# Row sums of the last two pairs of heads: exponentials of two steps added in place by VectorE

## The chip, the core and the metric

The kernel runs on one core of a Trainium2 chip. The metric is device microseconds (us) of one execution; less is better. The engines are named as the profile names them: PE (TensorE, matmuls), PEld (its weight loads), DVE (VectorE), ACT (ScalarE), POOL (GpSimd) and SP (SyncE, which here only issues DMAs). Each engine works through its own instructions in program order and waits on semaphores for the others. Matmul results stand in PSUM, everything else on the chip in SBUF.

## What is computed

A transformer block on x (2048 tokens of 512): layer norm, causal attention with 16 heads of 32, and a gated feed-forward layer; both results are added to x.

```python
q, k, v = (qkv[0], qkv[1], qkv[2])
scores = jnp.einsum('bhqd,bhkd->bhqk', q, k) * scale
scores = jnp.where(causal, scores, jnp.finfo(scores.dtype).min)
probs = jax.nn.softmax(scores, axis=-1)
attn = jnp.einsum('bhqk,bhkd->bhqd', probs, v)
...
x = x + _L0_attn_ref(xn, ...) + _L0_ffn_ref(xn, ...)
```

The change lies in the softmax's denominator: for each query the exponentials of all its scores have to be summed over the keys.

## The kernel before

**Tiling.** Queries come in 4 blocks of 512 (`qb`), keys in 16 tiles of 128 (`kt`). A *step* is one pair (`qb`, `kt`) of one head pair `p` (two heads; 8 pairs): scores with the 128 keys on partitions and the 512 queries on columns, their exponentials in a tile `prob` of 128 x 2 x 512 (two heads), and two products with them: with the values (`av`) and with a matrix of ones (`rows`), which gives the sums over the keys. Block `qb` has 4 `qb` steps *off the diagonal* (all keys lie before all queries) and 4 *diagonal* ones, d = 0 to 3, in which only 512 - 128 d columns are computed and a 128 x 128 triangle has to be cut out. There are 40 steps (`STEPS`).

**Stages.** After the projections a long loop (from line 820) takes six head pairs through 40 steps each. The stage that the change touches is the next one (lines 857 to 976): the last two pairs, 6 and 7, go through the 40 steps *together*, four heads at a time. Behind it comes the output projection (line 1147), then the feed-forward layer.

**One step of the together stage**, in the order in which it is written out by hand (lines 944 to 968), which is the order of each engine's queue:

- PE: `score_cols` (line 242) and `add_scores` (line 257) put the scores of four heads into four PSUM tiles. Each of the two pairs has three such tiles in rotation (`ps_t`, `ps_s`), two of them in one step, so a step's second tile needs the first exponential of the step before to be done with its own.
- PE: `run_due(s)` issues what earlier steps put off with `later_on(wait, ...)` to this step: `values_together` (line 895, four matmuls on four groups of 32 columns) and `rows_together` (line 909, likewise) of the step before.
- DVE, diagonal steps only: the scores of the triangle are cut at zero (line 880, four instructions).
- ACT: four exponentials (line 881), ordered head 0 of both pairs, then head 1. They write the step's two `prob` tiles, each with two heads.
- POOL, diagonal steps only: the triangle is cut out of each `prob` tile (line 286, two instructions).
- `keep_together`: at a block's end the value sums are copied by ACT (line 924) and the row sums by DVE (line 927); `normalize_attention` (lines 407 and 409: reciprocal on DVE, product on POOL) is done in eighths, one per step.

The order of the steps (`together`, line 861) is, for each block in the order 1, 0, 2, 3: diagonal d, then `qb` steps off the diagonal, for d = 0 to 3. The pool `probs` (line 796) has five buffers; the long loop uses it too, there with one tile per step, and the last matmuls that read such a tile are issued at most four steps after it.

In the long loop POOL already adds the exponentials of two steps (`add_up`, line 352), so that there one row-sum product serves two steps. In the together stage each step has its own.

Of the kernel before, what the change touches and what calls it, by code (L numbers as in the profile page):

```python
# [42 lines left out]
ALU = mybir.AluOpType  # L43
# [3 lines left out]
P = 128  # L47
# [33 lines left out]
def block_kernel(  # L81
# [10 lines left out]
    nc = tc.nc  # L92
# [8 lines left out]
    with (  # L101
# [39 lines left out]
        units, steps, first = [], [], {}  # L141
# [86 lines left out]
        def rows_when_due(beside_values=True):  # L228
            if due and tick[0] >= due[0][0]:
                rows_from_parts(beside_values)  # L230
            tick[0] += 1

        def score_cols(p, n, pool):

            qb, kt = steps[n]
            c0 = max(0, kt - 4 * qb) * P
            tiles = []
            for h in range(2):
                first = rows_of(p, h).start
                rows = slice(first, first + 3)  # L240
                ps = tile_of(pool, f"ps_t{p}_{n}_{h}")
                nc.tensor.matmul(  # L242
                    ps[:, c0:],
                    lhsT=ones_h[rows, :],
                    rhs=negs[p // 2, qb][rows, c0:],
                    start=True,
                    stop=False,
                )
                tiles.append(ps)
            return tiles  # L250

        def add_scores(p, n, tiles):
            qb, kt = steps[n]
            c0 = max(0, kt - 4 * qb) * P
            for h, ps in enumerate(tiles):
                rows = rows_of(p, h)
                nc.tensor.matmul(  # L257
                    ps[:, c0:],
                    lhsT=keys[kt // 4][rows, p // 2, (kt % 4) * P : (kt % 4 + 1) * P],
                    rhs=queries[qb][rows, p // 2, c0:],  # L260
                    start=False,
                    stop=True,
                )
# [21 lines left out]
        def omit_later_keys(diag):  # L285
            nc.gpsimd.affine_select(
                out=diag,
                in_=diag,
                compare_op=ALU.is_ge,
                fill=0.0,  # L290
                base=0,
                pattern=[[0, 2], [1, P]],
                channel_multiplier=-1,
            )
# [80 lines left out]
        def keep_attention():  # L375

            p, qb = full.pop(0)
            av, row = avs[p, qb], rows[p, qb]
            og, half = p // 2, slice(64 * (p % 2), 64 * (p % 2 + 1))
            if p % 2 == 0:  # L380
                sums[og, qb] = sump.tile([P, TB], F32, tag="sums", name=f"sums{og}_{qb}")
            if p >= NP - 2:
                copy = nc.vector.tensor_copy if p % 2 else nc.scalar.copy
                copy(aT[og][qb][half], av[:64])
                copy(sums[og, qb][half], row[64:])
            else:
                if qb == 0:
                    nc.scalar.copy(aT[og][qb][half], av[:64])
                else:
                    both = turn_tile(8 + p % 2, f"both{p}_{qb}")  # L390
                    nc.scalar.copy(both, av)  # L391
                nc.vector.tensor_copy(sums[og, qb][half], row[64:])
                if qb > 0:
                    other = slice(64 * (1 - p % 2), 64 * (2 - p % 2))
                    nc.scalar.copy(aT[og][qb][half], both[other])
                    nc.gpsimd.tensor_tensor(
                        aT[og][qb][half], aT[og][qb][half], both[half], ALU.add
                    )
            if p % 2 == 1:
                invert.extend((og, qb, i) for i in range(8))  # L400

        def normalize_attention():

            og, qb, i = invert.pop(0)
            cols = slice(i * (P // 2), (i + 1) * (P // 2))
            part = sums[og, qb][:, cols]
            nc.vector.reciprocal(part, part)
            dst = aT[og][qb][:, cols]
            nc.gpsimd.tensor_tensor(dst, dst, part, ALU.mult)
# [383 lines left out]
            tc.tile_pool(name="late", bufs=1, side="right", reuse_waits="tile")  # L793
        )
        attention = ExitStack()
        probs = attention.enter_context(tc.tile_pool(name="probs", bufs=5, reuse_waits="tile"))
        sump = attention.enter_context(tc.tile_pool(name="sums", bufs=5, reuse_waits="tile"))

        def turn_tile(i, name, dtype=F32, shape=(P, TB)):
# [13 lines left out]
        def later_on(wait, f, *args):  # L813
            todo.setdefault(at[0] + wait, []).append((f, args))

        def run_due(m):
            for f, args in todo.pop(m, []):
                f(*args)

        for m in range((NP - 2) * STEPS):  # L820
            p, n = divmod(m, STEPS)
# [12 lines left out]
            qb, kt = steps[n]  # L834
# [22 lines left out]
        together = []  # L857
        for qb in TOGETHER:
            mine = [n for n in range(STEPS) if steps[n][0] == qb]
            for d in range(4):  # L860
                together += [mine[4 * qb + d], *mine[d * qb : (d + 1) * qb]]

        def diagonal(n):
            return steps[n][1] >= 4 * steps[n][0]

        def exponentials_together(n, two):

            qb, kt = steps[n]
            c0 = max(0, kt - 4 * qb) * P
            both = [  # L870
                probs.tile([P, 2, TB], F32, tag="prob", name=f"prob{NP - 2 + i}_{n}")
                for i in range(2)
            ]
            for h in range(2):
                for i in range(2):
                    ps = two[i][h]
                    if diagonal(n):

                        diag = ps[:, c0 : c0 + P]
                        nc.vector.tensor_scalar(diag, diag, 0.0, None, ALU.min)  # L880
                    nc.scalar.activation(both[i][:, h, c0:], ps[:, c0:], AF.Exp)
            if diagonal(n):
                for i in range(2):
                    omit_later_keys(both[i][:, :, c0 : c0 + P])
            return both
# [19 lines left out]
        def rows_together(qb, exps, c0, first, last):  # L905
# [10 lines left out]
            if last:  # L916
                kept.append(("rows", qb))

        kept = []

        def keep_together():
            what, qb = kept.pop(0)
            if what == "values":
                nc.scalar.copy(aT[NOG - 1][qb], avs[NP, qb])
            else:
                sums[NOG - 1, qb] = sump.tile([P, TB], F32, tag="sums", name=f"sums_last{qb}")
                nc.vector.tensor_copy(sums[NOG - 1, qb], rows[NP, qb])
                invert.extend((NOG - 1, qb, i) for i in range(8))
# [5 lines left out]
        def load_rest(b, n):  # L934

            lm[b, n] = []
            for part in range(2):
                t = turn_tile(8 * ORDER.index(b) + 2 * n + part, f"lm{b}_{n}_{part}", F32R)
                nc.sync.dma_start(out=t.bitcast(F32), in_=kept_x[b][1 + part][:, n])
                lm[b, n].append(t)  # L940

        early_loads = [(ORDER[i], n) for i in range(2) for n in range(NK)]
        last_n = {steps[n][0]: n for n in together}
        for s, n in enumerate(together):
            at[0] = s
            rows_when_due()
            two = [score_cols(NP - 2, n, ps_t), score_cols(NP - 1, n, ps_s)]
            for i in range(2):
                add_scores(NP - 2 + i, n, two[i])
            if s == 0:  # L950
                for m in sorted(todo):
                    run_due(m)
            run_due(s)
            qb, kt = steps[n]
            both = exponentials_together(n, two)
            while full:
                keep_attention()
            while kept:
                keep_together()
            first = s == 0 or steps[together[s - 1]][0] != qb  # L960
            last = n == last_n[qb]
            later_on(1, values_together, n, both, first, last)
            exps = [both[j // 2][:, j % 2] for j in range(4)]
            later_on(1, rows_together, qb, exps, max(0, kt - 4 * qb) * P, first, last)
            if invert:
                normalize_attention()
            if early_loads and s > 4:
                load_rest(*early_loads.pop(0))
        assert not early_loads
        for m in sorted(todo):  # L970
            run_due(m)
        while kept:
# [117 lines left out]
    for n in range(NG * NC):  # L1090
        g, j = divmod(n + 1, NC)
        pieces += [(g, 0, j), (g, 1, j)] if g < NG else [None, None]
        g, j = divmod(2 * (n // 2 + 1) + n % 2, NC)
# [237 lines left out]
```

## Time and profile before

| what | us |
|---|---|
| three runs | 1923.87, 1920.15, 1920.36 (median 1920.36) |
| the profiled execution, its own time | 1925.87 |
| its span, first to last instruction | 1924.1 |
| the together stage, from its first scores to the first matmul of the output projection | 675.0 to 789.1 |
| mean granted TensorE clock | 0.995 |

How to read it. A line of a timeline gives start, length, engine, source line, operation, output <- inputs, the pattern and the number of merged instructions; in square brackets stands idle time of that engine and what ended it. A 32-bit matmul shows as two records, so the four matmuls of `rows_together` are x8. In a table by windows each engine has its busy time in that stretch. PE matmuls are pipelined: one starts before the record of the last has ended, so the time of a group of matmuls is taken from its start to the start of the next group.

### The profile page before, as it was taken

To read this page: it belongs to the slowest core of one execution; us is meant where nothing else is said; L and a number is where in the kernel's file an instruction comes from. 1 tells how busy PE (TensorE), PEld (TensorE's weight loads), DVE (VectorE), ACT (ScalarE), POOL (GpSimd) and SP (SyncE) were. 2 spreads that over 40 slices of the span, in tenths; PEclk is the share of its full clock that TensorE was granted. 3 is DMA by queue.
4 is the path that set the end of the run, shared out by engine and by line. 5 is a ranking of instruction groups with operands and counts; after the bars stand their busy time and mean duration, and the time that the engine had idled before them with its cause. 6 is when DMAs were issued, how large, how long until landed. Compare 5 with 4: busy or idle time off the path is not lost.

```text
span 1924.1 us, 32421 instructions
## 1 busy us (share of the span) xinstructions
PE 1902.7 (99%) x11981; PEld 1223.0 (64%) x11981; DVE 1325.8 (69%) x2772; ACT 1136.6 (59%) x2364; POOL 945.3 (49%) x1127
## 2 busy tenths in 40 slices
PE   9999999999999999999999999999999999999998
PEld 5666433333333332368888888888888888888886
DVE  7775667776776842348777777677777767777774
ACT  3643466666666666336666666666666666666554
POOL 3310265665665631236555645555555545555551
PEclk9999899999999999999999999999999999999999
DMA  5212000000000110630000000000000000000002
GB/s 197 107 48 88 1 2 2 1 2 2 2 2 2 51 40 2 198 105 24 20 20 21 21 19 21 20 20 20 21 21 19 24 19 19 20 23 19 19 5 88
DMA packets 52991, 65.01 MB, mean 34 GB/s; under 512 B 4960, under 2 KB 37728, under 8 KB 51296
## 3 DMA queue, kind: packets, MB, share of 16 engines
q1 hardware_dynamic: 52832, 62.93, 9.7%
q8 instruction: 94, 1.54, 0.3%
q14 instruction: 65, 0.53, 0.1%
HBM read 46.14 MB, written 16.78 MB: 33 GB/s over the span
## 4 chain that ended last, share of the span: by engine, by line
PE 92%; ACT 3%; POOL 2%; DVE 2%; issue 1%; DMA 0%; SPq 0%; DVEq 0%; ACTq 0%; POOLq 0%
PE gu L1183 25%; PE gu L1196 12%; PE pd L1246 12%; PE ps_s L165 8%; PE av L305 7%; PE pd L1258 6%; PE ps_t L242 4%; PE ps_t L257 3%; PE po L1150 3%; ACT prob L271 2%; PE av_last L895 2%; PE rows_last L909 1%; PE ps_k L592 1%; PE ps_v L592 1%; POOL added L357 1%; PE ps_q L592 1%
## 5 line engine op out<-in xcount | busy, mean ns | idle before, releaser
L1183 PE MATMUL gu<-xh,gu 128*128 128x512 f32 x1024 | 403.9, 394 | 0.0
L1183 PE MATMUL gu<-lm,gu 128*128 128x512 f32 x1024 | 403.6, 394 | 0.0
L189 DVE TENSOR_REDUCE tops<-ps_s 128x1 f32<-128x512 f32 x384 | 245.1, 685 | 112.8 <-PE ps_s L165 74.5
L1267 DVE SCALAR_TENSOR_TENSOR acc<-pd,acc 128x512 f32<-128x512 f32 x512 | 316.9, 680 | 2.4 <-PE pd L1258 2.4
L1228 POOL TENSOR_TENSOR parts<-inter,hi 128x512 fp32r<-128x512 f32 x128 | 171.3, 1338 | 278.8 <-DVE hi L1224 271.1
L165 PE MATMUL ps_s<-k,q 32*128 32x512 f32 (+3 forms) x1280 | 287.3, 583 | 0.0
L1220 DVE SCALAR_TENSOR_TENSOR inter<-gu,gate 128x512 f32<-128x512 f32 x128 | 88.5, 692 | 278.4 <-PE gu L1196 274.2
L1196 PE MATMUL gu<-lm,gu 128*128 128x512 f32 x1024 | 279.7, 395 | 0.0
L257 PE MATMUL ps_t<-q,k 32*128 32x512 f32 (+3 forms) x1280 | 270.5, 540 | 0.0
L1253 ACT ACTIVATE pd<-pd 128x512 f32<-128x512 f32 x512 | 263.2, 581 | 1.1 <-PE pd L1246 1.1
L1190 ACT ACTIVATE gu<-gu 128x512 f32<-128x512 f32 x256 | 148.6, 581 | 187.9 <-PE gu L1183 187.9
L1246 PE MATMUL pd<-wd,parts 128*128 128x512 f32 x1024 | 259.6, 396 | 0.0
L271 ACT ACTIVATE prob<-ps_t 128x512 f32<-128x512 f32 x288 | 156.3, 594 | 119.1 <-PE ps_t L257 95.9
L1196 PEld LDWEIGHTS gu<-lm,gu 128*128 128x128 f32 x1024 | 192.0, 188 | 47.1 <-issue 0.2
L1183 PEld LDWEIGHTS gu<-lm,gu 128*128 128x128 f32 x1024 | 191.9, 187 | 46.6 <-issue 0.2
L1246 PEld LDWEIGHTS pd<-wd,parts 128*128 128x128 f32 x1024 | 192.3, 188 | 45.8
L1183 PEld LDWEIGHTS gu<-xh,gu 128*128 128x128 f32 x1024 | 192.0, 188 | 45.7 <-issue 0.2
L357 POOL TENSOR_TENSOR added<-prob,prob 128x512 f32<-128x512 f32 x144 | 179.6, 1269 | 68.9 <-ACT prob L271 68.4
L305 PE MATMUL av<-prob,v 128*32 128x128 f32 (+3 forms) x1536 | 192.3, 404 | 4.2 <-ACT both L391 2.1
L1227 ACT CAST parts<-hi 128x512 fp32r<-128x512 f32 x128 | 79.8, 623 | 173.7 <-DVE hi L1224 170.2
L1048 POOL TENSOR_TENSOR w<-mag,sc 128x256 f32<-128x256 f16 x128 | 91.9, 739 | 166.5 <-DVE mag L1036 164.2
L184 DVE CUSTOM_DVE_ANT_0 ps_s<-ps_s,mask_qk 128x128 f32<-128x128 f32 (+3 forms) x256 | 120.7, 516 | 52.2 <-PE ps_t L257 26.1
(141 smaller groups left out, 3044.4 us busy)
## 6 DMA issues: line engine op xcount, KB each, us to landing
kx<-xp SPq DMA_DIRECT2D x12, 1024.0 KB, 6.2
pk<-packed SPq DMA_DIRECT2D x96, 128.0 KB, 2.1
lm<-kx SPq DMA_DIRECT2D x32, 256.0 KB, 4.9
x<-x SPq DMA_DIRECT2D x16, 256.0 KB, 5.6
acc<-x SPq DMA_DIRECT2D x16, 256.0 KB, 4.8
sc<-scales SPq DMA_DIRECT2D x64, 64.0 KB, 2.2
sc<-scales SPq DMA_DIRECT2D x32, 128.0 KB, 2.4
xh<-kx SPq DMA_DIRECT2D x16, 256.0 KB, 4.1
```

The lines of the kernel that those rows point to most:

```text
L165: nc.tensor.matmul(ps[:, :w], lhsT=queries[qb][rows, p // 2, i * P : (i + 1) * P], rhs=keys[c][rows, p // 2, :w], start=True, stop=True,)
L189: nc.vector.tensor_reduce(top, ps[:, :w], AX.X, ALU.max)
L257: nc.tensor.matmul(ps[:, c0:], lhsT=keys[kt // 4][rows, p // 2, (kt % 4) * P : (kt % 4 + 1) * P], rhs=queries[qb][rows, p // 2, c0:], star ...
L271: nc.scalar.activation(prob[:, h, :], ps, AF.Exp)
L305: nc.tensor.matmul(avs[p, qb][D * j : D * (j + 1), c0:c1], lhsT=vals[kt // 4][:, kt % 4, D * head : D * (head + 1)], rhs=prob[:, h, c0:c1] ...
L357: nc.gpsimd.tensor_tensor(t, prob_a[:, h], prob_b[:, h], ALU.add)
L1183: nc.tensor.matmul(ps, lhsT=parts[:, i, k], rhs=mov, start=(k == 0 and i == 0), stop=(k == NK - 1 and i == 1),)
L1196: nc.tensor.matmul(ps, lhsT=gu[g, m, j][:, 2, k], rhs=lm[b, k][1], start=False, stop=(k == NK - 1), skip_group_check=True,)
L1228: nc.gpsimd.tensor_tensor(parts[:, 1], inter, high, ALU.subtract)
L1246: nc.tensor.matmul(po, lhsT=parts[:, part, i * P : (i + 1) * P], rhs=w[:, part], start=(part == 0), stop=(part == 1),)
L1253: nc.scalar.activation(po, po, AF.Copy, scale=HIGH_SCALE)
L1267: nc.vector.scalar_tensor_tensor(acc[t], po, SUM_SCALE, acc[t], ALU.mult, ALU.add)
```

## The change

Off the diagonal, `older` and `newer` steps form couples. DVE adds the newer step's exponentials into the older step's `prob` tiles, in place, with four instructions (two pairs, two heads), and one group of four row-sum matmuls then serves both. The additions are written behind the next step's exponentials (and so behind its four cuts at zero, if that step is diagonal); the row sums of the couple are issued two steps after its second step, ahead of that step's values. The steps off the diagonal are regrouped so that couples stay whole: behind the diagonals d = 0 to 3 come 2, 0, 2, 0 steps in block 1; 2, 2, 2, 2 in block 2; 4, 2, 4, 2 in block 3. The first diagonal's row sums in a block are put off by two steps in place of one. The pool `probs` has six buffers in place of five.

```diff
-        probs = attention.enter_context(tc.tile_pool(name="probs", bufs=5, reuse_waits="tile"))
+        probs = attention.enter_context(tc.tile_pool(name="probs", bufs=6, reuse_waits="tile"))
...
             mine = [n for n in range(STEPS) if steps[n][0] == qb]
+            ends = [0] + [2 * -(-qb * d // 2) for d in range(1, 4)] + [4 * qb]
             for d in range(4):
-                together += [mine[4 * qb + d], *mine[d * qb : (d + 1) * qb]]
+                together += [mine[4 * qb + d], *mine[ends[d] : ends[d + 1]]]
...
+        def add_step(old, new):
+
+            for i in range(2):
+                for h in range(2):
+                    nc.vector.tensor_tensor(
+                        old[i][:, h], old[i][:, h], new[i][:, h], ALU.add
+                    )
+
...
+        held, adds = [], []
...
             both = exponentials_together(n, two)
+            while adds:
+                add_step(*adds.pop())
             while full:
                 keep_attention()
...
             later_on(1, values_together, n, both, first, last)
             exps = [both[j // 2][:, j % 2] for j in range(4)]
-            later_on(1, rows_together, qb, exps, max(0, kt - 4 * qb) * P, first, last)
+            if diagonal(n):
+                wait = 2 if first else 1
+                later_on(wait, rows_together, qb, exps, max(0, kt - 4 * qb) * P, first, last)
+            elif held:
+                older = held.pop()
+                adds.append((older, both))
+                exps = [older[j // 2][:, j % 2] for j in range(4)]
+                later_on(2, rows_together, qb, exps, 0, False, last)
+            else:
+                held.append(both)
...
         assert not early_loads
+        while adds:
+            add_step(*adds.pop())
         for m in sorted(todo):
             run_due(m)
```

## The prediction

> **What bounds the kernel now.** First the page's chain of work that ended last, then the busy times by windows for the together stage.
>
> ```profile
> PE 92%; ACT 3%; POOL 2%; DVE 2%; issue 1%; DMA 0%; SPq 0%; DVEq 0%; ACTq 0%; POOLq 0%
> ```
>
> ```profile
> core 0: us, PE busy (x) PEld busy (x) DVE busy (x) ACT busy (x) POOL busy (x), PEclk, DMA share, GB/s
> 677.60:789.10 111.50, 109.66 (x1121) 34.59 (x1117) 32.87 (x103) 74.96 (x166) 24.00 (x73) 1.00 0.08 25
> ```
>
> PE sets the end; in this stage it is busy 109.7 of 111.5 us at full clock, DVE 32.9. Moving row sums from PE to DVE looks free by these shares. Whether it is depends on when a sum is wanted, so next the timeline of PE, over a step off the diagonal and a diagonal one (d = 1).
>
> ```profile
> 750.42 0.39 PE L242 MATMUL ps_t<-neg,ones_h 3*128 3x512 bf16 x4
> 750.65 1.03 PE L257 MATMUL ps_t<-q,k 32*128 32x512 f32 x8
> 751.61 1.06 PE L895 MATMUL av_last<-prob,v 128*32 128x512 f32 x8
> 752.49 1.04 PE L909 MATMUL rows_last<-prob,ones 128*32 128x512 f32 x8
> 753.47 0.34 PE L242 MATMUL ps_t<-neg,ones_h 3*128 3x384 bf16 x4
> 753.64 0.81 PE L257 MATMUL ps_t<-q,k 32*128 32x384 f32 x8
> 754.38 1.06 PE L895 MATMUL av_last<-prob,v 128*32 128x512 f32 x8
> 755.27 1.04 PE L909 MATMUL rows_last<-prob,ones 128*32 128x512 f32 x8
> 756.24 0.40 PE L242 MATMUL ps_t<-neg,ones_h 3*128 3x512 bf16 x4
> ```
>
> From start to start: scores 1.19 us (diagonal d = 1: 0.91), values 0.88, row sums 0.97, of which 0.1 is the change-over to the next scores, so 0.86 to 0.88 is the row sums' own. The step takes 3.04 us and nothing stands idle. Beside it, on DVE, ACT and POOL (one fence each):
>
> ```profile
> 754.55 0.89 DVE L880 TENSOR_SCALAR ps_t<-ps_t 128x128 f32<-128x128 f32 x4 [7.83 <-PE ps_t L257]
> 755.36 1.77 DVE L407 RECIPROCAL sums_last<-sums_last 128x64 f32<-128x64 f32 x4
> ```
>
> ```profile
> 751.77 2.06 ACT L881 ACTIVATE prob<-ps_t 128x512 f32<-128x512 f32 x4 [0.98 <-PE ps_t L257]
> 754.89 1.64 ACT L881 ACTIVATE prob<-ps_t 128x384 f32<-128x384 f32 x4 [1.05 <-DVE ps_t L880]
> ```
>
> ```profile
> 756.22 0.79 POOL L286 TENSOR_SCALAR_AFFINE_SELECT prob<-prob 128x256 f32<-128x256 f32 x2 [9.09 <-ACT prob L881]
> ```
>
> To see: DVE is idle (7.83 us) until a diagonal step's scores end; its four cuts then hold the queue until 0.98 us after those scores (755.36 - 754.38). The next instruction in that queue will be an addition.
>
> **The change, part by part.** Sums are against this execution (span 1924.1, own time 1925.87, 5.5 above the median of the three runs); I add the difference to the median, 1920.36.
>
> *Removed:* 12 groups of row sums, 12 x 0.86 = 10.3 us of PE.
>
> *Added:* 48 additions of 128x512, two SBUF inputs. The nearest row is the same operation in the projections:
>
> ```profile
> 14.27 2.49 DVE L546 TENSOR_TENSOR xp<-xT,high 128x512 fp32r<-128x512 f32 x4
> ```
>
> Four take 2.49 us: about 0.60 apart, the last 0.69.
>
> *The wait this adds.* By program order a couple's additions stand behind the next step's cuts, and its row sums on PE behind the step after next's scores, ahead of that step's other products. Of the 12 couples 9 are followed by a diagonal step. Take d = 1, time 0 at the end of its scores. DVE: additions from 0.98, the fourth ends at 0.98 + 2.49 = 3.47, if POOL does not disturb. PE: values 0.88, change-over 0.1, scores 1.19: 2.17; the diagonal's second exponential (0.51 + 0.87 = 1.38) holds the second tile, so about 2.6. PE then stands until the fourth addition, and behind the fourth row-sum matmul stand that diagonal's values, its row sums and all later scores. The couple's own buffers wait as well: with six, the exponentials of that step write the tiles that the sums are read from.
>
> *POOL beside the additions.* The two cuts of the triangle (0.41 each by the row above) become due 1.8 us after the diagonal's scores (756.22 - 754.38), amid the additions. No addition and no such cut meet in this trace. The nearest meeting is in the projections, DVE first, then POOL:
>
> ```profile
> 51.98 2.54 DVE L460 SCALAR_TENSOR_TENSOR wp<-wh,raw_q 128x512 fp32r<-128x512 f32 x2
> ```
>
> ```profile
> 51.01 1.28 POOL L457 TENSOR_TENSOR wp<-raw_q,wh 128x512 fp32r<-128x512 f32 x1
> 52.25 1.73 POOL L546 TENSOR_TENSOR xp<-xt,hi 128x512 fp32r<-128x512 f32 x1
> ```
>
> Two DVE operations with two SBUF inputs took 2.54 us in place of 0.60 + 0.69 = 1.29, and POOL's second 1.73 in place of 1.28: they took turns. For a couple the bounds are 0 (the triangle's cut does not count) and 2 x 0.41 = 0.8; I take 0.3 for each cut, 0.6, near the upper end, since the only meeting in the trace shows full blocking and less than POOL's whole record (DVE's second operation ended 0.55 after POOL's, less than its own 0.69).
>
> The Trainium skill has the rule that speaks against this change ("SBUF — State Buffer", section "Who interferes with whom"): a DVE instruction with two SBUF inputs contends with a GpSimd instruction that reads SBUF, and whichever starts first holds the port for its whole length. The row above agrees for two arithmetic operations; for the triangle's cut no row shows it. By the rule the sum below stands or rises by up to 2 us; without it, it falls by 4.8.
>
> So the fourth addition ends at 3.47 + 0.6 = 4.07, its matmul starts at 4.12, and the row sums end their turn at 4.98.
>
> *Cycles* (diagonal and the two steps behind it; before: from scores to scores in the same timeline):
>
> - d = 1, three: before 2.77 + 2.62 + 3.04 = 8.43. After: 0.91 + 4.98 + values 0.65 + rows 0.65 + 0.12 = 7.31, then 1.19 + 0.88 + 0.1 = 2.17: 9.48. **+1.05**
> - d = 2, two: before 8.00. After 0.65 + 4.96 + 0.44 + 0.44 + 0.12 + 2.17 = 8.78. **+0.78**
> - d = 3, three: before 7.80. After 0.45 + 4.95 + 0.22 + 0.22 + 0.12 = 5.96, then 2.17 and 0.35 of waiting for an exponential that itself waited for the row sums: 8.48. **+0.68**
> - d = 0 of the last block, one: about 9.9 against 9.33, one triangle's cut among the additions. **+0.6**
>
> Together 3.15 + 1.56 + 2.04 + 0.6 = 7.35. Two couples precede another couple: additions start as soon as the exponentials are there, the row sums are in time, and 0.86 less 0.3 (scores now wait for ACT, whose four take 2.06 of a step of 2.17) is saved: -1.1. The last couple has no later step to hide under: its additions follow the last exponentials, the row sums follow them, and the output projection stands behind: about 1.0 more than the 4.1 us now from the last scores (784.97) to line 1150 (789.08). **Sum: +7.25.**
>
> *At nothing:* the other order by itself (PE has the same work; two diagonal steps meet in block 1, as they do in block 0 now: -0.3 to +0.7). The later row sums of a first diagonal (PE has other work there). The sixth buffer in the long loop: a tile's last matmul is issued four steps after it, so five already sufficed, and from 250 to 675 us every exponential before which ACT stood idle starts within 0.12 us of the end of some scores (0 to -1). The loads behind the stage wait for its last scores and have PE's 55 us at line 1150 to land in. The reciprocals go behind the additions; their eighths are wanted blocks later.
>
> **Rivals.**
>
> 1. *The additions are in time, faster.* Place: DVE's queue behind a diagonal's cuts. If the fourth addition ended by 2.6 us, PE would not stand: each cycle 4.12 - 2.71 = 1.4 shorter, nine: -12.6, so 7.25 - 12.6 = -5.4: 1915; without the waits for exponentials -10.3: 1910. The balance tips at 4.07 - 7.25 / 9 = 3.3 us. For it: DVE is idle 78.6 us of the stage. Against: even undisturbed 0.98 + 2.49 = 3.47.
> 2. *POOL and DVE do not meet:* 9 x 0.6 less: +1.85 (one cut less at d = 0: +2.1), 1922.
> 3. *They meet fully*, 0.8 a couple and a piece of line 409 (0.32): up to 9 x 0.5 = +4.7 more, 1932.
> 4. *It does nothing:* excluded as to the lists (48 row-sum matmuls less, 48 additions more), but PE may not set the stage's end as I think: 1920.
>
> **How the numbers follow.** Forecast 1920.4 + 7.2 = 1927.6, chance 0.60, its own range 1924.5 to 1931; rival 1 0.13, rival 2 0.15, rival 3 0.10, rival 4 0.02. About 0.2% (3.8 us) is what a measurement here tells from no change. Faster by more: 0.13, rival 1. Within: most of rival 2 and rival 4, 0.14. Slower: the forecast, rival 3 and the rest of rival 2, 0.73. The range leaves out rival 1 and the ends: 1921 to 1934.
>
> **What would show it.** Right: line 910 (row sums) with gaps ahead of it, ended by DVE's additions, about nine of 1 to 1.5 us, after diagonal steps only; additions longer than 0.69 where a triangle's cut runs; the stage 7 us longer, all else in place. Wrong: no gap at the row sums (rival 1), or additions of 0.69 throughout (rival 2); a change in the long loop would mean that the sixth buffer mattered.

## The result, and the profile after

| | before | after |
|---|---|---|
| median of 20 runs | 1920.22 us | 1924.44 us |
| profiled execution: own time, span | 1925.87, 1924.1 | 1926.91, 1925.2 |
| together stage, first scores to first matmul of the output projection | 675.00 to 789.08: 114.08 | 670.87 to 790.15: **119.28** |
| from there to the end of the span | 1135.1 | 1135.1 |

The ratio is 1.0026, with a 95% interval from 1.0018 to 1.0034: about 5 us slower. The two spans differ by 1.1 us only. The stretch ahead of the stage hides the rest: there the granted clock differs from one execution to the next. From 100 to 230 us it was 0.95 in the one before and 1.00 in the one after, and the stage began 4.1 us earlier. Whoever compares spans of single executions measures this too. The stage itself, at a granted clock of 1.00 in both, is 5.2 us longer, and behind it nothing has changed.

The chain of work and the window of the stage (from its second scores, as in the prediction), after:

```profile
PE 93%; ACT 3%; POOL 2%; DVE 1%; issue 1%; DMA 0%; SPq 0%; DVEq 0%; ACTq 0%; POOLq 0%
```

```profile
673.49:790.15 116.66, 114.47 (x1024) 36.62 (x1021) 65.55 (x151) 75.99 (x166) 31.75 (x73) 1.00 0.08 24
```

PE has 97 records fewer (x1121 to x1024; 48 matmuls of two records make 96) and yet 4.8 us *more* busy time. Its busy share is 98%, as before. By this line PE is simply busy; that it stands must be read from the timeline. PE after, a diagonal step d = 1 and the step behind it (the one shown before at 753.47):

```profile
754.80 0.34 PE L242 MATMUL ps_t<-neg,ones_h 3*128 3x384 bf16 x4
754.97 0.81 PE L257 MATMUL ps_t<-q,k 32*128 32x384 f32 x8
755.72 1.06 PE L896 MATMUL av_last<-prob,v 128*32 128x512 f32 x8
756.72 0.80 PE L242 MATMUL ps_t<-neg,ones_h 3*128 3x512 bf16 x4
757.15 1.23 PE L257 MATMUL ps_t<-q,k 32*128 32x512 f32 x8
758.30 1.96 PE L910 MATMUL rows_last<-prob,ones 128*32 128x512 f32 x7
759.65 0.88 PE L896 MATMUL av_last<-prob,v 128*32 128x384 f32 x6
760.10 0.75 PE L910 MATMUL rows_last<-prob,ones 128*32 128x512 f32 x4
...
761.91 0.39 PE L242 MATMUL ps_t<-neg,ones_h 3*128 3x512 bf16 x4
```

A group of row sums, eight records in 1.04 us before, now takes 1.96 us for seven of them. There is no gap: one matmul starts whenever an addition has ended, so the group is drawn out and counts as busy. The step takes 761.91 - 756.72 = 5.19 us. Why, on DVE and POOL, and in the list of waits of the stage (what waited, for what: us in all, times, longest):

```profile
755.89 0.89 DVE L881 TENSOR_SCALAR ps_t<-ps_t 128x128 f32<-128x128 f32 x4 [3.07 <-PE ps_t L257]
756.69 2.90 DVE L924 TENSOR_TENSOR prob<-prob,prob 128x512 f32<-128x512 f32 x4
```

```profile
757.55 1.50 POOL L286 TENSOR_SCALAR_AFFINE_SELECT prob<-prob 128x256 f32<-128x256 f32 x2 [4.33 <-ACT prob L882]
```

```profile
PEld rows_last L910 <- DVE prob L924: 16.7, 29, 0.8
ACT prob L882 <- DVE prob L924: 5.5, 7, 1.2
```

The additions stand behind the cuts (755.89, four in 0.89 us), as predicted; the four take 2.90 us, not 2.49, and the two triangle cuts 1.50, not 0.79. The fourth ends at 759.59, 3.8 us after the diagonal's scores (755.78). Weight loads of the row sums wait for additions 29 times. These 16.7 us are waits of single matmuls that partly lie beside each other, not time lost. The second line is the exponentials of the step behind: they wait to write a buffer that the additions still read. The values made from them are not drawn out (1.07 us at 763.10), so this wait shows no loss of its own here; more than six buffers were not tried.

### The profile page after: what moved, and what is told of

It is laid out like the page before. It is cut to its first block, busy times and chain, and to the rows that moved or that the text cites. A ratio compares the mean times of both kernels' runs of the same rounds, so it can differ in the third digit from the quotient of the medians.

```text
span 1925.2 us, 32270 instructions
## 1 busy us (share of the span) xinstructions
PE 1902.4 (99%) x11885; PEld 1224.6 (64%) x11885; DVE 1358.2 (71%) x2820; ACT 1137.2 (59%) x2364; POOL 953.7 (50%) x1127
## 4 chain that ended last, share of the span: by engine, by line
PE 93%; ACT 3%; POOL 2%; DVE 1%; issue 1%; DMA 0%; SPq 0%; DVEq 0%; ACTq 0%; POOLq 0%
PE gu L1206 25%; PE gu L1219 12%; PE pd L1269 12%; PE ps_s L165 8%; PE av L305 8%; PE pd L1281 6%; PE ps_t L242 4%; PE ps_t L257 3%; PE po L1173 3%; ACT prob L271 2%; PE av_last L896 2%; PE ps_k L592 2%; PE rows_last L910 1%; PE ps_q L592 1%; PE ps_v L592 1%; POOL added L357 1%
## 5 line engine op out<-in xcount | busy, mean ns | idle before, releaser
L165 PE MATMUL ps_s<-k,q 32*128 32x512 f32 (+3 forms) x1280 | 282.9, 576 | 0.0
```

The lines of the kernel that those rows point to most:

```text
L165: nc.tensor.matmul(ps[:, :w], lhsT=queries[qb][rows, p // 2, i * P : (i + 1) * P], rhs=keys[c][rows, p // 2, :w], start=True, stop=True,)
```

## The experiments

Since spans move with the clock ahead of the stage, each run is judged by the length of its together stage in its trace (same two ends; equal stretches agree to 0.02 us between kernels), with the ratio of the timed runs to the kernel before beside it. A cycle is a diagonal step and what follows up to the next. The granted clock within the stage was 1.00 in every run but e2. The ratios are looser than the stages, since the executions that they compare differ in mean granted clock (0.995 to 1.000): all six of e2 had 0.997 or less, more than half of those before 0.999 or 1.000.

| run | stage, us | ratio to before (95%) |
|---|---|---|
| before | 114.08 | 1 |
| changed kernel | 119.28 | 1.0026 (1.0018 to 1.0034) |
| e1, order alone | 114.13 | 1.0003 (0.9992 to 1.0015) |
| e2, additions first | 121.96 (3.4 us of it at half clock) | 1.0049 (1.0037 to 1.0061) |
| e3, no additions | 107.02 | 0.9972 (0.9960 to 0.9984) |
| e4, no triangle | 115.52 | 1.0003 (0.9992 to 1.0013) |
| e5, mask on VectorE | 115.48 | 0.9996 (0.9984 to 1.0007) |
| e6, mask, sums behind the values | 111.83 | 0.9979 (0.9968 to 0.9990) |
| e7, sums behind the values | 116.60 | 1.0015 (1.0004 to 1.0025) |
| e8, before with the mask | 113.16 | 0.9993 (0.9982 to 1.0004) |
| e9, as e6, one ahead | **107.76** | **0.9974 (0.9964 to 0.9985)** |
| e10, one ahead | 112.11 | 0.9989 (0.9978 to 1.0001) |
| e11, as e6, two ahead | 108.69 | 0.9979 (0.9970 to 0.9988) |
| e12, as e7, one ahead | 113.40 | 0.9999 (0.9988 to 1.0011) |

**Theory:** a couple's additions stand in DVE's queue behind the next diagonal's cuts, POOL's triangle cuts stretch them, and PE, in program order, stands at the row sums. **Rivals:** the new order or the sixth buffer costs the time; the additions are too long wherever they stand; something else than the sums holds PE, such as the exponentials that hold the scores' tiles.

**e1, the order and the buffers alone.**

```diff
-            if diagonal(n):
...
-                held.append(both)
+            later_on(1, rows_together, qb, exps, max(0, kt - 4 * qb) * P, first, last)
```

> The changed kernel's order of steps and its six exponential buffers, but row sums of every step as before, no additions. Theory (late sums are the loss): nothing to lose here, the together stage 114.1 us as in the kernel before, within -0.5 to +0.7. Rival (the order or the sixth buffer costs): the stage 116 to 119 us, a good part of the 5.2 us that the changed kernel lost there.

114.13: the first rival falls. This run has the changed kernel's order of steps, so cycles are compared with it below.

**e2, the additions ahead of the next step's cuts.**

```diff
+            while adds:
+                add_step(*adds.pop())
             both = exponentials_together(n, two)
-            while adds:
-                add_step(*adds.pop())
```

> The changed kernel with a couple's four additions put on VectorE's queue ahead of the next step's four cuts in place of behind them. Theory (the queue position behind a diagonal's cuts makes the sums late): the fourth addition ends some 2 us sooner, before the scores behind which its row sums stand have ended, so no gap at the row sums; but the diagonal's cuts, exponentials and triangle start up to 1.5 us later, and its values take over as the thing waited for. Net 0.2 to 0.5 us a cycle gained, the stage 115 to 117.5 us against 119.3. Rival (the queue position is not what matters, the additions' own length is): 119 us or more. If the diagonal's later exponentials cost nothing: 110 us.

121.96: missed, and on the wrong side. In this execution the granted clock fell to 0.50 inside the stage:

```profile
684.30:687.70 3.40, 3.40 (x26) 0.84 (x24) 2.17 (x7) 1.72 (x6) 2.12 (x7) 0.50 0.02 5
```

At half clock 3.4 us can hold 1.7 us too much, so at full clock the stage lies between 120.3 and 122.0, still at least 1.0 us longer than in the changed kernel. (In block 2 and later, far from that stretch, the cycles are 1.2 us longer in all.) By its number the rival (119 or more) is met, but not for its reason. The sums are early now (the fourth addition ends 1.8 us after the diagonal's scores, not 3.8), and additions and triangle cuts no longer meet (no addition over 0.69 us, every cut 0.41). But see PE, ACT and DVE at a diagonal d = 2, whose scores end at 725.24:

```profile
726.49 0.39 PE L242 MATMUL ps_t<-neg,ones_h 3*128 3x512 bf16 x1
727.78 0.65 PE L242 MATMUL ps_t<-neg,ones_h 3*128 3x512 bf16 x3 [0.91 <-ACT prob L882]
```

```profile
727.35 1.21 ACT L882 ACTIVATE prob<-ps_t 128x256 f32<-128x256 f32 x4 [1.89 <-DVE ps_t L881]
```

```profile
724.55 2.50 DVE L924 TENSOR_TENSOR prob<-prob,prob 128x512 f32<-128x512 f32 x4 [5.04 <-ACT prob L882]
726.96 0.89 DVE L881 TENSOR_SCALAR ps_t<-ps_t 128x128 f32<-128x128 f32 x4
```

The cuts start at 726.96, 1.7 us late. The exponentials wait 1.89 us for them, and the next scores, which need a tile that the diagonal's first exponentials read, stand from their first matmul (726.49) to 727.78, with PE empty for 0.91. I had named the diagonal's values as the next thing waited for; the scores' tiles come earlier. So the queue's place matters in both directions: behind the cuts the sums are late, ahead of them the scores.

**e3, no additions.**

```diff
-                nc.vector.tensor_copy(sums[NOG - 1, qb], rows[NP, qb])
+                nc.vector.tensor_scalar(
+                    sums[NOG - 1, qb], rows[NP, qb], 1e-20, None, ALU.max
+                )
...
-                adds.append((older, both))
```

> The changed kernel without the 48 additions; the row sums of a couple leave out its second step (a lower bound of 1e-20 keeps the sums from being zero). Theory: with nothing to wait for, the removed 12 x 0.86 us of row sums show nearly in full: the stage 104 to 107 us, 12 to 15 us less than the changed kernel, 1910 to 1913 us in all. Rival (something besides the additions stretches the stage: buffers, order, exponentials): the stage stays above 110 us.

107.02: all that the additions cost, waits and turns, is 119.28 - 107.02 = 12.3 us. The nine steps in which the sums of a couple meet a diagonal are 0.84 to 1.72 us shorter, 11.4 in all; the last step is 0.6 shorter. Against e1 the removed row sums show with 7.1 us, not 10.3, because PE, with less work, now runs into the exponentials. Behind a diagonal d = 1 the second scores wait until its exponentials leave their tiles (from the first scores at 712.13 to the row sums at 714.04 it is 1.91 us, where scores take 1.19). In a diagonal step d = 2 mostly the values of the step before wait for theirs (the step takes 2.20 us, its work is 0.65 + 0.88 + 0.12 = 1.65).

**e4, no triangle**, and **e5, the triangle as a mask in DVE's own cut** (e5's diff; e4 has the last three lines alone. `mask_kq`, made once ahead of everything, is 0 where a key may be seen and -3e38 elsewhere).

```diff
-                        nc.vector.tensor_scalar(diag, diag, 0.0, None, ALU.min)
+                        nc.vector.scalar_tensor_tensor(
+                            diag, diag, 0.0, mask_kq, ALU.min, ALU.add
+                        )
...
-            if diagonal(n):
-                for i in range(2):
-                    omit_later_keys(both[i][:, :, c0 : c0 + P])
```

> The changed kernel without GpSimd's cut of the triangle in the together stage, so later keys within a diagonal tile of 128 stay in. Theory (additions and triangle cuts take turns and make the sums later): all 48 additions take 0.68 us, the fourth ends 0.4 us earlier in each of nine cycles, the stage 3.5 to 5 us shorter, 114.5 to 116 us. Rival (they overlap without harm where it matters): the stage within 1 us of 119.3.

> The changed kernel with the triangle's cut of the together stage joined to VectorE's cut (minimum with zero plus a mask of -3e38 in one operation, ahead of the exponential), so GpSimd does none there; nothing left out. Theory (additions and GpSimd's cuts take turns, 0.41 us a cycle): all additions 0.68 us, the stage like the run without the triangle, 115 to 116.5 us (114.1 in the kernel before, 119.3 in the changed one). Rival (the joined cut costs VectorE more than the turns did): its four take over 0.1 us longer each, the stage 118 us or more.

115.52 and 115.48, within 0.05 of each other: without POOL's cuts the stage is 3.8 us shorter. Of this, 3.5 us lie in the nine steps in which a couple's sums meet a diagonal: 0.42 in each of eight, 0.21 at d = 0 of the last block, where only one cut comes among the additions. The additions of e4, by line (count, shortest, median and longest in ns), and who waited for them:

```profile
L921 DVE TENSOR_TENSOR prob<-prob,prob x48: 681/684/693, 684.8 to 787.9; 128x512 f32<-128x512 f32 x48
...
  PEld rows_last L907: 13.2, 26
```

None is long any more (in the changed kernel 17 of 48 take 0.88 to 0.89), and still 13.2 us of waits: position alone makes the sums late. The joined cut takes 0.29 us, like the plain one, so on DVE the mask is free.

**e6 and e7, a couple's row sums behind the diagonal's values**, with the mask and without.

```diff
+            while behind:
+                later_on(1, *behind.pop())
             if diagonal(n):
...
-                later_on(2, rows_together, qb, exps, 0, False, last)
+                behind.append((rows_together, qb, exps, 0, False, last))
```

The expectations say "behind the values and row sums" of the diagonal. This run does half of that: `while behind` stands ahead of the line that puts off the diagonal's row sums, so these still stand behind the couple's. The same holds for e9, e11 and e12.

> The same, and a couple's row sums put behind the values and row sums of the diagonal step in TensorE's order, in place of ahead of them. Theory (what is left is TensorE standing at row sums whose additions end 3.5 us after the diagonal's scores, with the diagonal's own products queued behind): those products are ready by 2 us now, fill the wait, and the additions are in time: the stage 107 to 109.5 us, near the 107.0 of the run without additions, 1913 to 1916 us in all. Rival (the scores' tiles, held by exponentials, are the bound, not the order): 114 us or more.

> The changed kernel with only the order of the last run: a couple's row sums behind the diagonal's products, the triangle still cut by GpSimd. Theory: GpSimd's cuts, stretched by the additions, end as late as the additions, so the diagonal's products wait in place of the row sums: the stage 118.5 to 120 us, no gain. Rival (the order alone is enough): under 115 us.

e6: 111.83, faster than the kernel before; it lies between the 107 to 109.5 expected and the rival's 114. PE and DVE at a diagonal d = 2 whose scores end at 716.38:

```profile
718.81 0.64 PE L906 MATMUL av_last<-prob,v 128*32 128x256 f32 x8
719.26 2.01 PE L920 MATMUL rows_last<-prob,ones 128*32 128x512 f32 x16
```

```profile
717.26 2.48 DVE L934 TENSOR_TENSOR prob<-prob,prob 128x512 f32<-128x512 f32 x4
```

The diagonal's values (128x256) no longer wait, but the couple's row sums (128x512) come next, the fourth addition ends only at 719.74, and the diagonal's row sums stand behind them: the 16 records of both are drawn out over 2.01 us. With the diagonal's row sums ahead as well (0.44 us, from 719.26 on), the couple's would have begun at about 719.70 and hardly waited. By this estimate some 0.5 us of each such cycle is lost to the half-done order; no run shows it. e7: 116.60, between the loss expected (118.5 to 120) and the rival's 115. The diagonal's values do wait for GpSimd's cut now (PE's weight loads, stage; 4.6 us, 5 times in the changed kernel):

```profile
PEld av_last L896 <- POOL prob L286: 16.0, 21, 1.2
```

but they still fit ahead of the couple's last sum. The wait changed its name and became smaller.

**e8, the mask in the kernel before** (the edit of e5 in the old code).

> The kernel before, with the triangle's cut joined to VectorE's cut as in the first of these runs. Theory (TensorE is the bound there and no addition meets the cut): the stage 113 to 114.2 us, no more than 1 us gained. Rival (the cut on GpSimd held up this stage too, so the gain of the other runs is not the couples'): under 112 us.

113.16: 0.9 us, all of it in the first cycle of each block and in block 0; from d = 1 on, blocks 1 to 3 are as before. So what e5 gained in the cycles in which two cuts come among the additions is from the couples' turns, not from the old kernel's triangle. At d = 0 of the last block (0.21 there, 0.16 here) the two cannot be told apart.

**e9, e10, e11: one or two additions ahead of the cuts, the others behind.** (`PARTS` lists a couple's four additions. The diff is that of e9 and e10; e11 takes `[:2]` and `[2:]`, in another order of the four. e10 has this edit alone, e9 and e11 have that of e6 as well.)

```diff
+            for old, new in adds:
+                add_step(old, new, PARTS[:1])
             both = exponentials_together(n, two)
             while adds:
-                add_step(*adds.pop())
+                add_step(*adds.pop(), PARTS[1:])
```

> The mask on VectorE and the couple's row sums behind the diagonal's products, and the first of a couple's four additions put ahead of the next step's cuts, the other three behind them. Theory (there TensorE still stands some 0.5 us at the last row sum of a couple, because the fourth addition ends 3.38 us after the diagonal's scores; VectorE is idle just before the cuts, and the first addition's operands are ready by then): the additions end 0.60 us sooner at no price to the cuts, the stage 111.8 - 9 x 0.45 = 107.5 to 108.5 us, 1912 to 1914 us in all. Rival (the rest of the loss is the scores waiting for exponentials): 111 us or more.

> The changed kernel with only that: its first addition ahead of the cuts, GpSimd's triangle and the order of the row sums as in the changed kernel. Theory (the place in VectorE's queue is what makes the sums late, one addition is 0.60 us of it): 9 x 0.6 = 5.4 us less, the stage 113.5 to 115.5 us against 119.3. Rival (taking turns with GpSimd sets when the additions end, wherever they start): 117.5 us or more.

> As the first of these runs, but two additions ahead of the cuts (the first half of each tile of exponentials, in the order in which they come). Theory (what the diagonal's cuts lose comes back at the scores of the step behind, whose second tiles wait for the diagonal's first exponentials, as in the run with all four ahead): the second addition ends 0.45 us after the cuts could have begun, so up to 0.45 us a cycle lost: the stage 109.5 to 112 us. Rival (cuts may wait at no price): within 0.5 us of the run with one ahead.

e9: 107.76, as expected, 0.7 above the run without any addition and 6.3 below the kernel before (5.0 by the ratio). One ahead with the mask, but in the changed kernel's order of row sums, was not run. The same place as in e6 (scores end at 719.40):

```profile
721.83 0.64 PE L906 MATMUL av_last<-prob,v 128*32 128x256 f32 x8
722.29 1.47 PE L920 MATMUL rows_last<-prob,ones 128*32 128x512 f32 x16
```

```profile
718.60 0.69 DVE L935 TENSOR_TENSOR prob<-prob,prob 128x512 f32<-128x512 f32 x1 [3.12 <-ACT prob L895]
719.42 0.89 DVE L892 SCALAR_TENSOR_TENSOR ps_t<-ps_t,mask_kq 128x128 f32<-128x128 f32 x4
720.23 1.89 DVE L935 TENSOR_TENSOR prob<-prob,prob 128x512 f32<-128x512 f32 x3
```

One addition fits into DVE's idle time ahead of the cuts, which still start as the scores end, and the row sums take 1.47 in place of 2.01.

e10, the changed kernel with that edit alone: 112.11, 7.2 us less, more than the 5.4 expected from 9 x 0.60. With three additions left behind the cuts, only 11 are stretched, not 17; six meetings of 0.2 us are gone as well, and 9 x 0.60 + 6 x 0.20 = 6.6. The last 0.6 us are unexplained. PE's weight loads wait 6.7 us for additions (29 waits became 14):

```profile
L925 DVE TENSOR_TENSOR prob<-prob,prob x48: 679/686/893, 675.6 to 777.3; 128x512 f32<-128x512 f32 x48
...
  PE av_last L896: 12.8, 4
...
  PEld rows_last L910: 6.7, 14
```

e11: 108.69, 0.9 more than e9. Both sides missed: two ahead do cost something, but about 0.1 us a cycle, not up to 0.45. Whether the cuts' waiting or the other order of the additions costs it, this run does not separate.

**e12, one ahead and the couple's sums behind the diagonal's values, without the mask.**

> One addition ahead of the cuts and the couple's row sums behind the diagonal's products, with the triangle still cut by GpSimd: the fastest run so far without its mask. Theory (taking turns with GpSimd stretches the last additions and, by that, also holds the diagonal's own products): between the run with one addition ahead alone (112.1 us) and the one with the mask (107.8): 109.5 to 111 us. Rival (with the place in the queue and the order right, the turns are hidden and the mask is not needed): under 108.5 us.

113.40: both sides missed, since it is *slower* than e10. PE behind a diagonal:

```profile
725.79 0.63 PE L896 MATMUL av_last<-prob,v 128*32 128x256 f32 x4
726.60 0.41 PE L896 MATMUL av_last<-prob,v 128*32 128x256 f32 x2 [0.18 <-POOL prob L286]
```

The additions are in time here (1.4 us of waits for them in the whole stage), but the diagonal's values, now ahead, wait for the second triangle cut, which POOL ends at 726.54, later than the fourth addition (726.28). The order that gains 2.7 us alone and 3.7 with the mask loses 1.3 here: which of two late things should stand first depends on which is later.

## Why the prediction was right, and where its terms were off

1927.6 was forecast against 1920.4, +7.2; measured +5.0 by the ratio and +5.2 by the stage. The long loop gave back a little, as allowed for: from its first scores to the stage it took 457.9 us with five buffers (e8) and 457.4 with six (after, e1, e6, e7 and e10) where the granted clock from 100 to 230 us was 1.00, and 462.9 (before) against 462.5 (e5) where it was 0.95. The mechanism held in each part: additions behind the cuts, PE standing at the row sums behind diagonals only, turns with POOL, nothing from the order. By cycles, the changed kernel against e1, which has the same order of steps:

| term | predicted | measured |
|---|---|---|
| d = 1, three | 3.15 | 1.27 + 0.85 + 0.87 = 2.99 |
| d = 2, two | 1.56 | 0.80 + 0.79 = 1.59 |
| d = 3, the first two | 1.36 | 0.68 + 0.38 = 1.06 |
| d = 3, the last, with the end | 0.68 + 1.0 | 1.68 |
| d = 0 of the last block | 0.6 | 0.56 |
| two couples ahead of a couple | -1.1 | -0.59 - 0.47 = -1.06 |
| d = 0 that begins blocks 1 and 2 | none | -0.85 - 0.85 = -1.70 |
| sum | 7.25 | 5.12 |

- **The step that failed** is the list of cycles. A removed group of row sums drops out of its couple's own cycle, the wait for the couple comes in the next one; I booked both where the wait is. Where cycles follow each other that is the same, but the first cycles of blocks 1 and 2 have the removed group and no wait: -1.7, of the 2.1 us by which the forecast's sum is too high. I had costed what changes there (the first diagonal's later row sums) at nothing. The reverse case, d = 3 of block 1 with a wait and no removed group, agrees by accident: the new wait partly took the place of an old one (the second step of block 0 took 4.47 us in e1, 2.96 in the changed kernel).
- **d = 3** was 0.3 us too dear where it fell short: in block 2 that cycle took 8.17 us, not 8.48, so the 0.35 us of waiting for an exponential did not show there. By the list of waits those exponentials stood for the additions (5.5 us in the stage), not for the row sums as assumed. The last cycle agrees only as a sum: from the end of the last scores to the output projection the changed kernel took 4.66 us (785.49 to 790.15), against 4.11 in the kernel before and 4.01 in e1. So the end cost 0.55 to 0.65, not 1.0, and what lies ahead of it about 1.0, not 0.68; that the two sizes make up for each other is luck.
- **Turns with POOL:** 0.6 a couple was taken, 0.42 measured (e4, e5). The fourth addition ends 3.8 us after the scores, not 4.07; undisturbed it ends after 3.4 (e4, e6), where I had 3.47. The Trainium skill ("SBUF — State Buffer", section "Who interferes with whom") says that a two-input DVE instruction and a GpSimd instruction that reads SBUF contend; the runs show it for the triangle's cut as well. The price is smaller than a whole cut for each meeting: 0.2 us on the addition.
- **The tipping point** was put at 3.3 us. Ending at 3.4 (e5) the stage is still 1.4 us longer than before; ending at 2.9 (e10) it is 2.0 shorter. It lies between, near 3.2.
- **Rival 1** (faster, 1910 to 1915) needed additions in time, and e9 is that case: 6.3 us less. It took the mask and another order of the row sums too; e10, with the place in the queue alone, gains 2.0. Rivals 2 and 3 fall by the 0.42, rival 4 by e1 and e3.
- "At nothing": the order held (0.05 us); the sixth buffer was tried with the order only, and together they cost nothing in the stage.
- **What to look for** was put wrongly in one point: no gaps appear ahead of line 910. PE counts as busy while it waits, and only drawn-out groups and the list of waits show it.

## What to carry to other kernels

Work taken from a full engine and given to an idle one pays only if its result is ready when the full engine reaches it. Ask at which place of the idle engine's queue the new work stands, what it waits behind, and what then waits behind it: here all four additions behind the cuts lost 5 us, all four ahead lost 6 to 8, and one ahead and three behind gained 2. Judge so small an effect by the length of its stage in the trace, at an equal granted clock, compared step by step with a run that has the same order, and count in which steps the removed work stood.

## What the runs showed of the hardware that was not expected

- Where they meet, additions and triangle cuts alternate: in one cycle of the changed kernel (d = 2) additions started at 724.255, 724.854 and 725.456, 0.60 apart, and with the cuts there the next came 0.81 later, at 726.270. The addition's record grows from 0.68 to 0.89 us, the cut's from 0.41 to mostly 0.85 (0.58 to 0.90 in the changed kernel): POOL's records grow more than DVE's.
- PE's busy share says little about a wait when its matmuls go to four column groups: 98% before and after, while nine steps lost 0.84 to 1.72 us each to the additions.
- An addition in place waits also for the matmuls that still read its tile. In all 12 couples of e10 the first addition starts 0.07 to 0.19 us after the end of the older step's values (the profile names them in four); in the cycle of e2 shown above 0.2 us after them, and 0.56 after the exponential that it reads. An addition into a tile of its own was not tried.
- The granted clock of one stretch far ahead differs between executions and moves the start of the stage nearly as much as the whole effect of the change. With 1.00 from 100 to 230 us the long loop takes 457.4 us up to the stage (six buffers; after, e1, e6, e7, e10), with 0.96 461.1 to 461.3 (e2, e3, e4, e9, e11, e12), with 0.95 462.5 (e5).
